# Moving two NF4 steps, four weight splits and two query sums around the first attention steps of a fused cross-attention and feed-forward kernel

## The chip, the cores and the metric

The kernel runs on one core of one Trainium2 chip. The metric is the device time of one launch in microseconds (us). The core has a matrix engine (PE, with its weight loads shown apart as PEld), a vector engine (DVE), a scalar engine (ACT), GpSimd (POOL) and a queue that only issues DMA transfers (SP). Each engine works through its own instructions in the order in which the program emits them, and waits where an operand or a buffer is not ready.

## The reference

Eight sequences of 128 rows and 512 columns pass through one transformer block. Cut to what matters:

```python
# x, ctx: (8, 128, 512); 32 query heads share 8 key/value heads; head size 128
q = rope((layernorm(x) @ Wq).reshape(b, t, 32, 128))
k = rope((ctx @ Wk).reshape(b, t, 8, 128))
v = (ctx @ Wv).reshape(b, t, 8, 128)
logits = 30 * tanh(einsum(q, k) * 0.0884 / 30)     # grouped heads: 4 queries per key head
weights = softmax(where(mask, logits, -1e30))
x = x + (weights @ v).reshape(b, t, 4096) @ Wo
# feed-forward with weights that are quantized and dequantized (NF4, blocks of 64) on the way
dq = lambda w: NF4_CODE[searchsorted(bounds, w / absmax)] * absmax
h = silu(layernorm(x) @ dq(w1).T) * (layernorm(x) @ dq(w2).T)      # 1376 hidden
x = x + h @ dq(w3).T
```

## The kernel before

Every matrix product is made of three matmuls on operands that are split into a rounded part and a remainder (`split`: ACT casts the high part, line 155; DVE or POOL subtracts to get the low part, line 156; `product`, line 172, issues for each pair of operands high x low, high x high, low x high).

The program is one long list written out in the order of Python's loops; no scheduler reorders it. It has four stretches.

- **The head**, the loop over `tiles` with index n from 0 to 35 (line 631): key, value and first query projections, one PE tile each. Beside them run the layer norm of x, its transposes, and from n = 15 on the NF4 stream.
- **The attention steps**, the loop over i from 0 to 63 (line 762). A step i takes one of eight sequences and one of eight key/value heads (`where`). In it are queued on PE, in this order: the query projection of a later step (`q_proj`, bank "q"), the output projection of step i-3 (`project`), the transposes of the attention result of step i-2 (`turn`, tile `pt_a`, bank "q"), the products with the values of step i-1 (`values`, tile `pv`) and the scores of step i (`scores`, tile `pl`). Steps 0 to 2 are special: step 0 has two query projections (tiles 1_0 and 1_1), step 1 has one (1_2) and step 2 has one (1_3); step 3 has none. `project` begins in step 3.
- **The gate and up products** of the feed-forward (line 859) and **the down products** (line 872).

The NF4 work is a generator, `quantize`. One unit of it is one bound: ACT compares (line 196, 128x1024) and DVE accumulates (line 202, or 200 for the first bound of a block). `pump(n)` adds n to a credit and runs the stream until the credit is used, so that the order of the stream never changes, only where in the program its parts stand. On the way the stream issues loads of weights and of scales (`load`, `begin`, line 265 and 275), the reduction of the block maxima (`find`, lines 177 to 179), a normalization on POOL (line 206) and a closing product on DVE (line 280).

The query projection ends in `rope`: two copies on ACT (lines 463 and 464), a product with the cosine on DVE (line 465), a product with the sine on POOL (line 466) and the sum (line 467). For the second set of queries (u = 1: tiles 1_0 to 1_3) the cosine product is written back into the PSUM bank, and the sum runs on DVE and reads that bank; so the bank is free only when the sum is done. There are two banks with the tag "q", used in turn, in program order: 1_0, 1_1, 1_2, 1_3, then `pt_a` of step 2, `pt_a` of step 3, and so on. `pt_a` of step 2 thus takes the bank of tile 1_2, and `pt_a` of step 3 that of tile 1_3.

`q_proj` returns a function that emits the copies and products of `rope`; that one returns the sum as another function. In steps 1 and 2 the copies and products are emitted at the step's start (`later = [f() for f in later[:1]]`), and the sum after `scores`.

The four slices of the output weights of head group 0 (`wo` 0 to 3) are loaded ahead of the loop by `load_o(0, g)` and split when their entry in `due` comes up at the end of a step. The loads of later weights reuse their raw buffers, three with the tag "raw": the load of the first projection weights of the next group (`raw_wq` 1_0, issued in step 0, split at the end of step 2) waits until `wo` 1 is split, the next two for `wo` 2 and 3.

Of the kernel before, what the change touches and what calls it, by code (L numbers as in the profile page):

```python
# [23 lines left out]
G = NH // NKV  # L24
# [38 lines left out]
def block_kernel(ctx: ExitStack, tc: tile.TileContext, x, ctxt, mask, wq, wk, wv, wo, w1, w2, w3, w12t, w3_t,  # L63
                 rope_tab, nf_bias, out):
    nc = tc.nc
    V, S, Q, E = nc.vector, nc.scalar, nc.gpsimd, nc.tensor
# [9 lines left out]
    def bank(tag, name):  # L76
        shape = [P, 1024 if tag == "pv" else 512]
        return ps.tile(shape, F32, tag=tag, name=name, bufs=2 if tag == "q" else 1)[:, :512]
# [75 lines left out]
    def split(hi, lo, src, engine):  # L154
        S.copy(hi, src)  # L155
        engine.tensor_tensor(lo, src, hi, ALU.subtract)  # L156
# [54 lines left out]
    class Down(Unit):  # L211
# [30 lines left out]
        def store(self, h):  # L242
            pool, tag, bufs = (f1, "w3t", 8) if h < 8 else (nf, "nf_t", 2) if h < 10 else (xp, "wide", 2)
            t = w3t[h] = pool.tile([P, 2, KT, P], F32R, tag=tag, name=f"w3t_{h}", bufs=bufs)
            own = t.rearrange("p i k c -> p i (k c)")[:self.p].rearrange("p i (c e) -> p i e c", e=4)
            split(own[:, 0], own[:, 1], self.part(self.w, h).rearrange("p (e c) -> p e c", e=4), Q)
# [158 lines left out]
    def pump(n):  # L405

        credit[0] += n
        while credit[0] > 0:
            credit[0] -= next(stream, n + credit[0])
# [7 lines left out]
    def end_store():  # L417
        if stored:
            stored.pop()()
# [7 lines left out]
    with ExitStack() as c1:  # L427
# [11 lines left out]
        def stage(src, shape, name):  # L439
            if early:  # L440
                raw = early.pop(0)
            else:
                raw = raw_pool[-1].tile([P, 512], F32, tag="raw", name=f"raw_{name}", bufs=3 if len(raw_pool) > 1 else 4)
            if len(shape) == 3:
                raw = raw.rearrange("p (k n) -> p k n", k=shape[1])
            nc.sync.dma_start(raw, src)
            return raw
# [21 lines left out]
        wqt, todo = {}, {}  # L469

        def load_q(kv, g):
            wqt[kv, g], todo["q", kv, g] = columns(wq, kv * G + g, f"wq_{kv}_{g}")

        def q_proj(u, g):
            kv, half = divmod(u, 2)
            if g == 0:
                qr[u] = a1.tile([P, 4, G, T], F32, tag="qr", name=f"qr_{u}", bufs=2)
            pq = bank("q", f"pq_{u}_{g}")
            w, t = wqt[kv, g], xT[half]
            product(pq, [((w[:, 0, k], w[:, 1, k]), (t[:, 0, k], t[:, 1, k])) for k in range(KT)])  # L480
            return lambda: rope(qr[u][:, :, g, :], pq, cosq, sgnq, f"q{u}_{g}", V if u < 2 else None, u == 1)


        with ExitStack() as c3:
# [110 lines left out]
            def advance(n):  # L595

                while True:
                    while loads and (early or len(ready) < 4) and loads[0][0] < n + 7:
                        when, what, i, j = loads.pop(0)
                        ready.append((when, load[what](i, j)))  # L600
                    if not ready or ready[0][0] > n:
                        return
                    ready.pop(0)[1]()
# [27 lines left out]
            for n, (what, i, j) in enumerate(tiles):  # L631
                done = evac() if evac else None
                evac = make[what](i, j)
                if last:
                    last()
                last = done
                advance(n)
                end_store()
                for f in plan[n]:
                    f()  # L640
                if 9 <= n < 19:
                    store()
                if n >= 33:
                    store("wo")
                if n >= 15 and n != 17:
                    pump(1)
            last()
            evac()()
            for f in plan[len(tiles)]:
# [7 lines left out]
        def load_o(kv, g):  # L657
            h = kv * G + g
            raw = stage(wo[h * HD:(h + 1) * HD], [P, D], f"wo_{kv}_{g}")
            t = wot[kv, g] = at.tile([P, 2, D], F32R, tag="wo", name=f"wo_{kv}_{g}", bufs=8)  # L660
            todo["o", kv, g] = lambda: split(t[:, 0], t[:, 1], raw, Q if kv else V)

        def load_kv(kv):
            for half in range(2):
                krt[kv, half] = at.tile([P, 512], F32, tag="kr", name=f"krt_{kv}_{half}", bufs=4)
                nc.sync.dma_start(krt[kv, half], kr_d[kv, half])
            vt[kv] = at.tile([P, B, HD + 1], F32, tag="v", name=f"vt_{kv}")
            nc.sync.dma_start(vt[kv][:, :, :HD], v_d[kv])
            Q.memset(vt[kv][:, :, HD:], 1.0)

        def where(i):
            u, bb = divmod(i, 4)
            return u, u // 2, (u % 2) * 4 + bb, bb

        def scores(i):
            u, kv, b, bb = where(i)
            pl = bank("s", f"pl_{i}")
            E.matmul(pl, krt[kv, u % 2][:, bb * T:(bb + 1) * T], qr[u][:, bb].rearrange("p g t -> p (g t)"),  # L678
                     start=True, stop=True)
            th = at.tile([P, 512], F32, tag="th", name=f"th_{i}", bufs=3)  # L680
            S.activation(th, pl, AF.Tanh, scale=ATTN_MULT / CAP)  # L681
            S.activation(th, th, AF.Exp, scale=CAP)  # L682
            em[i] = th.rearrange("p (g t) -> p g t", g=G)
            Q.tensor_tensor(em[i], em[i], mt.unsqueeze(1).to_broadcast([P, G, T]), ALU.mult)  # L684

        def values(i):
            u, kv, b, bb = where(i)
            ad[i] = at.tile([P, G, HD], F32, tag="ad", name=f"ad_{i}")
            pv = ps.tile([P, G, 256], F32, tag="pv", name=f"pv_{i}", bufs=1)
            for g in range(G):  # L690
                E.matmul(pv[:, g, :HD + 1], em[i][:, g], vt[kv][:, b], start=True, stop=True)  # L691
            rs = tp.tile([P, G], F32, tag="rs", name=f"rs_{i}")
            V.reciprocal(rs.unsqueeze(2), pv[:, :, HD:HD + 1])
            V.tensor_tensor(ad[i], pv[:, :, :HD], rs.unsqueeze(2).to_broadcast([P, G, HD]), ALU.mult)
# [14 lines left out]
        for g in range(G):  # L709
            load_o(0, g)  # L710
# [41 lines left out]
                V.tensor_tensor(hT[half, h // 4][:, h % 4], sg, pu, ALU.mult)  # L752
            return later

        due = {0: [("o", 0, 0), ("o", 0, 1)], 1: [("o", 0, 2), ("o", 0, 3)]}
        xn = {}

        def turned(ks, tags):
            for f in [normal2(k, xn[k], tag) for k, tag in zip(ks, tags)]:
                f()  # L760

        for i in range(N):
            u, kv, b, bb = where(i)
            s8 = i % 8
            if kv + 1 < NKV:
                if s8 == 0:
                    load_kv(kv + 1)
                if s8 < 4:
                    load_q(kv + 1, s8)
                else:  # L770
                    load_o(kv + 1, s8 - 4)
                due.setdefault(i + (2 if i < 4 else 1), []).append(("q" if s8 < 4 else "o", kv + 1, s8 % 4))
            tiles = {0: (0, 1), 1: (2,), 2: (3,), 3: ()}.get(i, (bb,)) if u + 1 < 2 * NKV else ()
            later = [q_proj(u + 1, g) for g in tiles]
            later = [f() for f in later[:1]] + later[1:]
            if i == 0:
                later.pop(0)()
            if i > 3:
                store()
                end_store()  # L780
            pump(1.5 if 2 < i < 58 else 1 if i == 58 else 0)
            if 0 <= i - 3:
                project(i - 3)
            if i in (59, 61):
                ln = LayerNorm((i - 59, i - 58), f"y{i - 59}")
            if 0 <= i - 2:
                turn(i - 2)
            if 59 <= i < 63:
                ln.sums(i - 59)
            if 0 <= i - 1:  # L790
                values(i - 1)
            scores(i)
            if i == 0:
                later = [later[0]()]
            if i == 61:
                xn.update({k: pair.rows(k, "xn") for k in (0, 1)})
            for f in later:
                f()
            pump(1.65 if 2 < i < 58 else 2 if i == 58 else 1 if i < 2 else 0)
            if i == 62:  # L800
                turned((0, 1), "qq")
            if i in (60, 62):
                ln.finish(Q)
                pair = ln
            for k in due.pop(i, ()):
                todo[k]()
            if i >= 61:
                load_w12(i - 61)
# [63 lines left out]
    for b, i in down:  # L872
# [5 lines left out]
        for h in range(4 * i, min(NHT, 4 * i + 4)):  # L878
            m = min(P, H - h * P)
            t, s = w3t[h].rearrange("p i k c -> p i (k c)"), hs[b, i]  # L880
# [7 lines left out]
        elif i == 2:  # L888
            o = f1.tile([P, D], F32, tag="o", name=f"o_{b}", bufs=4)
# [41 lines left out]
```

## Time and profile before

| what | value |
|---|---|
| median of 3 runs | 789.06 us (788.82 to 789.34) |
| the profiled execution | 790.01 us, of which the span from its first to its last instruction is 788.2 us |
| PE busy | 778.0 us, 99% of the span |
| DVE, ACT, POOL busy | 627.9, 586.4 and 466.4 us |
| line 202 (DVE), line 196 (ACT) | 1196 and 1115 ns each on average |
| line 467 on POOL, line 684 on POOL | 1295 and 1310 ns each on average |
| mean granted PE clock | 0.998 |

PE's busy share counts pipelined matmuls whose ends are modelled, so a matmul that stalls in the array looks busy; where a stretch matters, the start times of its instructions say more than the share. Times given as positions are microseconds from the start of the span.

### The profile page before, as it was taken

Reading aid. Unit: us, or ns where it says so; the run is one execution under the profiler, and the core shown is the slowest. Engines: PE = TensorE matmul, PEld = TensorE weight load, DVE = VectorE, ACT = ScalarE, POOL = GpSimd, SP = SyncE. Lnnn points to the kernel's source line nnn. Section 1 sums busy time; section 2 is a strip of 40 time slices with the busy share of each in tenths; the row PEclk is TensorE's granted clock in tenths of the full one; section 3 lists DMA queues with packets and bytes.
Section 4 is the critical chain, followed back from the end, with each engine's and each line's share of the span. In section 5 each row is a group of like instructions: output and inputs, shape, how many; then the busy total and the mean of one; then the engine's idle time right before and its main releaser. Section 6 shows DMA issues by size and latency. Waiting matters only on the chain. (4 is left out here: it accounts for less than half of the span.)

```text
span 788.2 us, 11198 instructions
## 1 busy us (share of the span) xinstructions
PE 778.0 (99%) x3737; PEld 627.3 (80%) x3737; DVE 627.9 (80%) x840; ACT 586.4 (74%) x821; POOL 466.4 (59%) x411
## 2 busy tenths in 40 slices
PE   8999998999999999999999999999999999999998
PEld 6788886778777878778787877888778888888877
DVE  5767777888888887888888878879878688888981
ACT  7358667989796978879797979898732678778840
POOL 3568544688787878777797877878652223232100
PEclk9999999999999999999999999999999999999999
DMA  7966735355437344526337432414133235652011
GB/s 228 300 195 195 214 105 154 108 143 176 89 121 206 135 107 121 174 55 218 103 100 203 131 94 94 125 65 134 43 119 107 57 108 157 186 162 53 5 54 54
DMA packets 73329, 102.44 MB, mean 130 GB/s; under 512 B 7832, under 2 KB 42840, under 8 KB 73272
## 3 DMA queue, kind: packets, MB, share of 16 engines
q1 hardware_dynamic: 70104, 90.19, 38.2%
q0 software_dynamic: 3168, 11.54, 4.7%
q8 instruction: 30, 0.49, 0.3%
q14 instruction: 27, 0.22, 0.1%
HBM read 79.32 MB, written 22.38 MB: 129 GB/s over the span
## 5 line engine op out<-in xcount | busy, mean ns | idle before, releaser
L202 DVE SCALAR_TENSOR_TENSOR nc_w<-nm_w,nc_w 128x1024 f32<-128x1024 bf16 (+1 forms) x238 | 284.6, 1196 | 60.2 <-ACT nm_w L196 49.8
L196 ACT ACTIVATE nm_w<-w_w,bias 128x1024 bf16<-128x1024 f32 (+1 forms) x255 | 276.2, 1115 | 14.9 <-DVE nc_w L202 7.9
L172 PE MATMUL pq<-xT,wq 128*128 128x512 f32 x768 | 209.3, 422 | 0.0
L172 PE MATMUL po<-wo,aT 128*128 128x512 f32 x768 | 190.1, 396 | 0.0
L172 PEld LDWEIGHTS pq<-xT,wq 128*128 128x128 f32 x768 | 143.9, 188 | 55.9 <-issue 24.4
L172 PEld LDWEIGHTS po<-wo,aT 128*128 128x128 f32 x768 | 143.8, 189 | 34.5 <-issue 2.9
L684 POOL TENSOR_TENSOR th<-th,mt 128x512 f32<-128x512 f32 x64 | 83.8, 1310 | 87.9 <-ACT th L682 80.0
L466 POOL TENSOR_TENSOR rs_q<-rs_q,sgnq 128x512 f32<-128x512 f32 x64 | 82.9, 1295 | 14.7 <-ACT rs_q L464 14.7
L681 ACT ACTIVATE th<-pl 128x512 f32<-128x512 f32 x64 | 38.3, 598 | 53.5 <-PE pl L678 51.3
L467 POOL TENSOR_TENSOR qr<-rc_q,rs_q 128x512 f32<-128x512 f32 x56 | 72.5, 1295 | 0.0
L691 PE MATMUL pv<-vt,th 128*128 128x129 f32 x512 | 67.9, 276 | 0.1
L678 PE MATMUL pl<-qr,krt 128*128 128x512 f32 x128 | 66.4, 601 | 0.0
L172 PE MATMUL pg<-xT,w 128*128 128x512 f32 x264 | 63.7, 390 | 0.0
L172 PE MATMUL pu<-xT,w 128*128 128x512 f32 x264 | 63.5, 389 | 0.0
L691 PEld LDWEIGHTS pv<-vt,th 128*128 128x128 f32 x512 | 62.2, 192 | 0.7 <-POOL th L684 0.7
L172 PE MATMUL pd<-w3t,hs 128*128 128x512 f32 (+3 forms) x297 | 60.8, 366 | 0.4 <-POOL w3t L156 0.4
L172 PEld LDWEIGHTS pd<-w3t,hs 128*128 128x128 f32 (+1 forms) x297 | 51.3, 189 | 9.9 <-POOL w3t L156 0.8
L206 POOL TENSOR_TENSOR w_w<-w_w,s_w 128x1024 f32<-128x1024 f32 (+1 forms) x17 | 39.6, 2329 | 33.0 <-DMA s_w<-scale_d 31.6
L172 PEld LDWEIGHTS pu<-xT,w 128*128 128x128 f32 x264 | 49.6, 188 | 10.3
L172 PEld LDWEIGHTS pg<-xT,w 128*128 128x128 f32 x264 | 49.3, 188 | 10.1
L156 POOL TENSOR_TENSOR w3t<-w_w,w3t 128x512 fp32r<-128x512 f32 (+1 forms) x11 | 17.2, 1564 | 65.7 <-ACT w3t L155 65.7
L155 ACT CAST aT<-pt_a 128x512 fp32r<-128x512 f32 x64 | 36.6, 571 | 24.9 <-PE pt_a L162 24.9
(119 smaller groups left out, 1103.7 us busy)
## 6 DMA issues: line engine op xcount, KB each, us to landing
w12t_d<-dqt SPq DMA_DIRECT2D x22, 512.0 KB
w<-w12t_d POOLq DMA_DIRECT2D x22, 512.0 KB, 4.6
s_w<-scale_d SPq DMA_DIRECT2D x40, 256.0 KB
raw_wq<-in_L_xattn_Wq SPq DMA_DIRECT2D x32, 256.0 KB
raw_wo<-in_L_xattn_Wo SPq DMA_DIRECT2D x32, 256.0 KB
s_w<-scale_d SPq DMA_DIRECT2D x86, 64.0 KB
ws<-in_L_ffn_w SPq DMA_DIRECT2D x20, 256.0 KB
w_w<-in_w12t SPq DMA_DIRECT2D x10, 512.0 KB
```

The source lines that it names most:

```text
L155: S.copy(hi, src)
L156: engine.tensor_tensor(lo, src, hi, ALU.subtract)
L172: E.matmul(out, a, b, start=start and i + j == 0, stop=stop and i == n - 1 and j == 2)
L196: S.activation(m, self.w, AF.Relu, bias=bias[:self.p, i:i + 1], scale=BIG if up else -BIG)
L202: V.scalar_tensor_tensor(self.c, m, step, self.c, ALU.min, ALU.subtract if i == POS[0] else ALU.add)
L206: Q.tensor_tensor(self.w, self.w, self.s, ALU.mult)
L466: Q.tensor_tensor(s, s, every(sgn), ALU.mult)
L467: return lambda: (engine or Q).tensor_tensor(dst, c, s, ALU.add)
L678: E.matmul(pl, krt[kv, u % 2][:, bb * T:(bb + 1) * T], qr[u][:, bb].rearrange("p g t -> p (g t)"), start=True, stop=True)
L681: S.activation(th, pl, AF.Tanh, scale=ATTN_MULT / CAP)
L684: Q.tensor_tensor(em[i], em[i], mt.unsqueeze(1).to_broadcast([P, G, T]), ALU.mult)
L691: E.matmul(pv[:, g, :HD + 1], em[i][:, g], vt[kv][:, b], start=True, stop=True)
```

## The change

The diff moves work and removes none. In the head, `pump` runs two units instead of one at n = 24 and n = 28. The one unit at the end of each of steps 0 and 1 goes, so that the stream stands at the same place from step 2 on. The splits of `wo` 0 and 1, at the end of step 0 before, and of `wo` 2 and 3, at the end of step 1 before, now all stand in step 1: 0 and 1 ahead of `scores`, 2 and 3 at its end. The low parts of 2 and 3 are subtracted on POOL instead of DVE. The sums of tiles 1_2 and 1_3 are emitted straight after `values` instead of after `scores`. `scores` itself holds no DVE instruction.

```diff
@@ head, loop over n
                 if n >= 15 and n != 17:
-                    pump(1)
+                    pump(2 if n in (24, 28) else 1)
@@ load_o
-            todo["o", kv, g] = lambda: split(t[:, 0], t[:, 1], raw, Q if kv else V)
+            todo["o", kv, g] = lambda: split(t[:, 0], t[:, 1], raw, Q if kv or g > 1 else V)
@@
-        due = {0: [("o", 0, 0), ("o", 0, 1)], 1: [("o", 0, 2), ("o", 0, 3)]}
+        due = {1: [("o", 0, g) for g in range(G)]}
@@ loop over i
             if 0 <= i - 1:
                 values(i - 1)
+            if i in (1, 2):
+
+                later.pop(0)()
+                if i == 1:
+                    for _ in range(2):
+                        todo[due[1].pop(0)]()
             scores(i)
...
             for f in later:
                 f()
-            pump(1.65 if 2 < i < 58 else 2 if i == 58 else 1 if i < 2 else 0)
+            pump(1.65 if 2 < i < 58 else 2 if i == 58 else 0)
```

## The prediction

> **What bounds the kernel now.** I read the page first, then PE's waits, then a table of stretches, then the timeline of all engines around the one wait that is long. The page says that PE is busy all along, and the waits of PE say where it is not:
>
> ```profile
> PE 778.0 (99%) x3737; PEld 627.3 (80%) x3737; DVE 627.9 (80%) x840; ACT 586.4 (74%) x821; POOL 466.4 (59%) x411
> ```
> ```profile
> PE pt_a L162 <- DVE qr L467: 2.4, 1, 2.4
> PE warm L91 <- POOL ident masks.py:199: 1.4, 1, 1.4
> ```
>
> All other waits of PE sum to about 3 us in pieces of at most 0.5. The time is PE's queue, and only a change in when PE issues can move it. The one long wait is that of the first `pt_a`, for the sum (L467) of query tile 1_2. The table of stretches, cut at 3.41 us, shows what follows it (columns: stretch, length, busy us of PE, PEld, DVE, ACT, POOL, granted clock, DMA share, GB/s):
>
> ```profile
> 123.92:127.33 3.41, 2.99 (x12) 2.13 (x12) 3.41 (x4) 3.34 (x6) 2.21 (x2) 1.00 0.00 0
> 127.33:130.74 3.41, 1.38 (x13) 1.41 (x14) 3.38 (x6) 2.81 (x6) 2.07 (x2) 1.00 0.71 183
> 130.74:134.15 3.41, 3.41 (x8) 1.66 (x7) 3.38 (x7) 1.49 (x3) 0.39 (x2) 0.50 0.66 184
> 134.15:137.57 3.42, 3.42 (x22) 2.98 (x22) 2.54 (x3) 2.92 (x4) 2.36 (x2) 1.00 0.12 25
> ```
>
> PE worked 1.38 of 3.41 us, and in the next 3.41 us the granted clock is 0.50. DVE meanwhile is full. The timeline shows with what:
>
> ```profile
> 121.76 1.27 POOL L466 TENSOR_TENSOR rs_q<-rs_q,sgnq 128x512 f32<-128x512 f32 x1
> ...
> 123.68 1.22 DVE L202 SCALAR_TENSOR_TENSOR nc_w<-nm_w,nc_w 128x1024 f32<-128x1024 bf16 x1
> 123.91 3.00 PE L172 MATMUL pq<-xT,wq 128*128 128x512 f32 x12
> ...
> 124.81 2.39 DVE L156 TENSOR_TENSOR wo<-raw_wo,wo 128x512 fp32r<-128x512 f32 x2
> ...
> 125.12 1.53 POOL L466 TENSOR_TENSOR rs_q<-rs_q,sgnq 128x512 f32<-128x512 f32 x1 [2.08 <-ACT rs_q L464]
> 126.61 1.71 POOL L684 TENSOR_TENSOR th<-th,mt 128x512 f32<-128x512 f32 x1
> 127.12 0.69 DVE L465 TENSOR_TENSOR pq<-pq,cosq 128x512 f32<-128x512 f32 x1
> ...
> 128.53 0.68 DVE L467 TENSOR_TENSOR qr<-pq,rs_q 128x512 f32<-128x512 f32 x1
> ...
> 129.36 0.63 PE L162 MATMUL pt_a<-ident,ad 128*128 128x128 f32 x4 [2.44 <-DVE qr L467]
> ...
> 131.60 4.69 PE L172 MATMUL po<-wo,aT 128*128 128x512 f32 x12
> ```
>
> One NF4 unit and two `wo` splits (123.68 to 127.12) stand on DVE ahead of the rope of tile 1_2.
>
> **Part 1: what is taken out from ahead of the wait.** PE up to tile 1_3 (start 123.91) hangs on the sum of 1_1 at 123.07, itself after POOL's L466 of 121.76; nothing of the change stands before these. Undisturbed, a tile takes 2.85 (109.49 to 112.34), so PE is free for `pt_a` at 126.75. New ACT order: copies of 1_2 when PE has made it, 121.93 to 123.10; two casts of `wo` (0.6 each); tanh and exp of step 1 to 125.53; the other two casts to 126.55; copies of 1_3 126.95 to 128.12. New DVE order: L465 123.68 to 124.38, L693 and L694 to 125.18, the sum of 1_2 once POOL's L466 (123.17 + 1.28 = 124.45) is done: 125.10 to 125.78. The bank is free 0.9 before PE asks. Gain: 129.36 - 126.75 = 2.61. The next late thing could be pv of step 1, on L684: 125.60 + 1.29 = 126.89, wanted at 127.19, so it holds by 0.3.
>
> **Part 2: from this `pt_a` to the next.** Before: 129.36 to 136.13, 6.77. Undisturbed it is 4.52: 1.79 from `pt_a` to the next long group (143.82 to 145.61 in step 4) plus 2.73 of `po` (148.78 to 151.51). The excess of 2.25 is half of 3.41 us at clock 0.50, 1.7, and waiting of `po` for the low part of aT (L156, 132.62 to 133.30). In the new order PE would idle about 1.2 of 3.41 us at most (below); the start of the kernel has a stretch (4.46 to 7.87) with 2.64 busy of 3.41 at clock 1.00. I take it that the clock stays.
>
> [...]
>
> **Part 3: what is late next.** DVE and POOL hinder each other when DVE subtracts two SBUF operands: the two `wo` splits at 124.81 took 2.39 together, 0.69 and then 1.7 beside POOL's L466, and POOL's L684 right behind took 1.71 instead of 1.29. The second split ended 0.55 after L466, and L684 1.13 after the split. So they go one after the other. New order from 125.60: POOL L684 to 126.89; DVE `wo` 0 asked for at 125.70, done 127.44; POOL `wo` 2 done 128.57; DVE `wo` 1 done 129.12; POOL `wo` 3 done 130.25, L466 of 1_3 about 131.6. DVE: L465 of 1_3 129.04 to 129.73, low part of aT 129.65 to 130.33, L693 and L694 to 131.1, the sum of 1_3 131.65 to 132.35. PE: `pt_a` 126.75, pv 127.19, pl 128.08, first `po` 128.8, its third matmul waits for aT to 130.4, ten at 0.228 remain: free at 132.66; the bank of 1_3 is free at 132.5. [...] Both give **132.6 for the second `pt_a`**, an excess of 1.33 instead of 2.25, and a gain of 136.13 - 132.6 = **3.5**. Bounds: with POOL's three pieces at 1.29 and nothing between, 126.89 + 3.87 + 0.85 = 131.6, gain 4.5; with each at 1.71, the sum comes at 132.9 and L684 of step 2, a fourth piece, at 133.7, so that pv starts 0.4 late: gain 2.8. I take 3.5, from the rows of the same pairing.
>
> **Part 4: the moved load.** `raw_wq` 1_0 now waits for `wo` 1 until 129.12 (issued at 127.22 before). The load of this size issued at 136.54 shows in the DMA share of 137 to 139 and not after: 2.5 at most, so it lands by 131.6. ACT's cast then waits 1.2, which holds up behind it two L196, the cast of aT and tanh of step 3; POOL's split of it ends near 134.25. PE's next query tile starts at 134.4, and needs the low part third. Without that margin it would cost what it is late, one to one. Everything from there to the end shifts: ACT waited for PE's scores in 54 of 64 steps (51.3 us together), so it has slack in each, and the tail is `pd` on PE with 0.4 of waiting.
>
> **Part 5: the head.** Two more units at n = 24 and 28: 2 x (L196 1.15 + L202 1.22). They bring forward a reduction (1.21), the POOL normalization (2.40), L280 (1.21) and the DMAs of scales and `ws` on SP. Cover: between 72 and 112 PE waits for nothing; ACT has gaps of 0.6 to 1.7 before most copies, DVE of 0.8 to 1.5; POOL stands idle from 91.1 to 95.8, where the normalization goes; SP from 101.6 to 111.2, where the scales' load of step 0 goes, ahead of no waiting load. A value tile's bank is asked for again 2 tiles later, and the copy of n = 24 ends at 81.2 instead of 80.6, wanted at 85.7. Cost 0; up to 4.7 if nothing of it were covered; a gain is excluded, since PE has no wait there.
>
> **Sum.** The profiled execution has a span of 788.2 and a time of 790.0, 1.8 around it; the median of the runs is 0.95 below. Span 784.7, profile 786.5, median 789.06 - 3.5 = **785.5**. What a measurement here can tell from no change is 0.2%, 1.6 us: 787.5 to 790.6.
>
> **Rivals.**
> 1. *The clock halves all the same*, since the idle of 1.2 (or another cause) suffices. For it: no run here shows the limit between 2.64 and 1.38 us of work per stretch. Against: the clock fell exactly once, behind the one long wait. It gives back 1.7: 787.3. Chance 0.10, half of it counted as no change.
> 2. *Slower: ACT stands in step 2 behind the load of `raw_wq` 1_0.* After landing, the cast, two L196, an L202 and L705 (4.7 together) must be done before PE's second `po` at 137.57; so 3.7 from issue to landing cost nothing, and each us more costs one. [...] For: the load is issued 1.9 later than before, and the page's 512 KB loads on POOL's queue take 4.6. Against: the DMA share above. Chance 0.07.
> 3. *The head's two units are not covered.* One pair exposed (2.4) gives 787.9, both 790.2, no change either way. For: at 115.25 a weight load waits 0.32 for L465, so there the head is tight. Against: there the number of units is the same as before. Chance 0.05.
> 4. *The change does not do what it says*: the wait has another end than L467 and stays: 789. The releaser is named and the bank's order bears it out. Chance 0.01.
>
> **How the numbers follow.** The forecast has 0.77, with a range of its own of 784.5 to 786.3 (gains 4.5 to 2.8). To hold 8 in 10 it must reach rival 1 with some spread: 784.4 to 787.8. Faster: 0.77 + 0.05 = 0.82. No change: 0.05 + 0.05 + 0.01 = 0.11. Slower: 0.07.
>
> **What would show it.** Right: the wait of `pt_a` for L467 of 2.4 is gone, the first `pt_a` starts near 126.8, no stretch at clock 0.50 after the start, the second `pt_a` near 132.6, and `po` before it has a hole of about a microsecond ended by aT's L156 or, at `pt_a`, by L467; the head's PE times up to 118 agree within 0.3. Wrong: a clock of 0.50 near 131 (rival 1), ACT waiting for a DMA at the wq cast beyond 133 (rival 2), PE's first score later than 118.1 (rival 3), or a shift at the second `pt_a` that is not kept at the last `pd`.

## The result, and the profile after

The changed kernel takes 786.20 us in the median (785.79 to 786.97, 6 runs), the kernel before on the same chips 789.27 (788.82 to 789.84, 6 runs): a ratio of 0.9959, with a 95% interval of 0.9949 to 0.9969. That is 3.1 us less, where 3.5 was forecast. The profiled execution took 786.97, its span 785.2 (788.2 before).

PE's waits, the kernel after (what waited, for whom: us in total, times, longest):

```profile
PE warm L91 <- POOL ident masks.py:199: 1.4, 1, 1.4
PE pk L172 <- DVE rc_k L465: 0.9, 2, 0.7
PE po L172 <- DVE aT L156: 0.7, 1, 0.7
```

The wait of `pt_a` for L467 is gone; a wait of `po` for aT's low part has come. The same stretches as before:

```profile
123.92:127.33 3.41, 3.38 (x16) 2.54 (x16) 3.38 (x6) 2.87 (x7) 2.37 (x3) 1.00 0.03 8
127.33:130.74 3.41, 2.70 (x17) 1.76 (x16) 3.38 (x6) 2.93 (x5) 3.41 (x3) 1.00 0.26 61
130.74:134.15 3.41, 3.41 (x21) 2.93 (x22) 2.29 (x3) 2.67 (x5) 3.41 (x3) 1.00 0.51 170
```

No stretch at 0.50. In the first two stretches DVE is as full as before (3.38), and POOL now works without a break from 127.1 to 134. The timeline after, all engines, the rows that answer to those of before:

```profile
122.11 2.69 POOL L466 TENSOR_TENSOR rs_q<-rs_q,sgnq 128x512 f32<-128x512 f32 x2
...
125.43 0.68 DVE L467 TENSOR_TENSOR qr<-pq,rs_q 128x512 f32<-128x512 f32 x1
...
126.03 3.33 DVE L156 TENSOR_TENSOR wo<-raw_wo,wo 128x512 fp32r<-128x512 f32 x2
...
127.10 0.60 PE L162 MATMUL pt_a<-ident,ad 128*128 128x128 f32 x4
127.10 3.41 POOL L156 TENSOR_TENSOR wo<-raw_wo,wo 128x512 fp32r<-128x512 f32 x2
...
129.89 0.68 DVE L156 TENSOR_TENSOR aT<-pt_a,aT 128x512 fp32r<-128x512 f32 x1
...
130.62 2.58 PE L172 MATMUL po<-wo,aT 128*128 128x512 f32 x10 [0.71 <-DVE aT L156]
...
133.03 0.60 PE L162 MATMUL pt_a<-ident,ad 128*128 128x128 f32 x4
```

The sum ends at 126.11, a microsecond before PE asks for the bank. What is late next is aT's low part, behind two DVE splits that take 3.33 together.

Positions in a span move by some tenths from run to run: the first scores (`pl`) start between 117.7 and 118.6 in the twelve profiles here, and the difference is there from the first `pt_x` on, which stands 53.3 to 53.4 ahead of them in all. So the experiments are compared by one distance, from the start of the first scores to the start of the second `pt_a`: 136.13 - 118.12 = 18.0 before, 133.03 - 118.45 = 14.6 after. From the second `pt_a` to the end of the span, all twelve profiles lie between 652.1 and 652.3: whatever happens in steps 0 to 3 is kept to the end in full, and nothing is given back.

### The profile page after: what moved, and what is told of

Same layout as the page of the kernel before. It is cut to its first block, busy times and chain, and to the rows that moved or that the text cites. A ratio compares the mean times of both kernels' runs of the same rounds, so it can differ in the third digit from the quotient of the medians.

```text
span 785.2 us, 11201 instructions
## 1 busy us (share of the span) xinstructions
PE 777.0 (99%) x3737; PEld 627.3 (80%) x3737; DVE 628.3 (80%) x838; ACT 586.3 (75%) x821; POOL 469.1 (60%) x413
## 5 line engine op out<-in xcount | busy, mean ns | idle before, releaser
L202 DVE SCALAR_TENSOR_TENSOR nc_w<-nm_w,nc_w 128x1024 f32<-128x1024 bf16 (+1 forms) x238 | 284.6, 1196 | 57.0 <-ACT nm_w L196 46.1
L196 ACT ACTIVATE nm_w<-w_w,bias 128x1024 bf16<-128x1024 f32 (+1 forms) x255 | 276.0, 1115 | 15.9 <-DVE nc_w L202 7.9
L684 POOL TENSOR_TENSOR th<-th,mt 128x512 f32<-128x512 f32 x64 | 83.5, 1305 | 87.2 <-ACT th L682 78.7
L466 POOL TENSOR_TENSOR rs_q<-rs_q,sgnq 128x512 f32<-128x512 f32 x64 | 82.5, 1289 | 15.0 <-ACT rs_q L464 14.8
L467 POOL TENSOR_TENSOR qr<-rc_q,rs_q 128x512 f32<-128x512 f32 x56 | 72.5, 1294 | 0.0
```

What stands on the lines that cost most here:

```text
L196: S.activation(m, self.w, AF.Relu, bias=bias[:self.p, i:i + 1], scale=BIG if up else -BIG)
L202: V.scalar_tensor_tensor(self.c, m, step, self.c, ALU.min, ALU.subtract if i == POS[0] else ALU.add)
L466: Q.tensor_tensor(s, s, every(sgn), ALU.mult)
L467: return lambda: (engine or Q).tensor_tensor(dst, c, s, ALU.add)
```

## The experiments

The theory: PE waits in steps 1 to 3 for a chain of DVE and POOL instructions, and each piece ahead of the sum of 1_2 and of aT's low part is paid for. Rivals: the moved NF4 units alone do it; the half clock is a cost of its own, or has a cause of its own.

| kernel | distance | PE waits by its list: for the first `pt_a`, for aT in `po` | ratio to before, 95% interval |
|---|---|---|---|
| before | 18.0 | 2.4, none listed (half clock) | 1 |
| changed | 14.6 | none, 0.7 | 0.9959 (0.9949 to 0.9969) |
| nf4_only | 15.9 | 1.3, 0.5 | 0.9976 (0.9966 to 0.9985) |
| splits_only | 16.6 | none, 0.5 (high part) and 1.3 | 0.9992 (0.9983 to 1.0001) |
| sum_behind_splits | 15.1 | 1.3, none | 0.9966 (0.9954 to 0.9978) |
| filled_wait | 17.6 | 0.2, 1.1 | 0.9999 (0.9990 to 1.0007) |
| wo_all_dve | 15.8 | none, 1.9 | 0.9983 (0.9974 to 0.9992) |
| no_pool_splits | 13.8 | none, none | 0.9951 (0.9937 to 0.9964) |
| one_ahead | 13.8 | none, none | 0.9952 (0.9939 to 0.9964) |
| interleaved | 13.6 | none, none | 0.9948 (0.9936 to 0.9960) |

**nf4_only**, the NF4 units alone:

```diff
-                    pump(1)
+                    pump(2 if n in (24, 28) else 1)
...
-            pump(1.65 if 2 < i < 58 else 2 if i == 58 else 1 if i < 2 else 0)
+            pump(1.65 if 2 < i < 58 else 2 if i == 58 else 0)
```

> Only the two NF4 units move into the head; splits and sums stand as in the kernel before. Worked from rows: without the two L202 the sum of 1_2 ends near 127.1, so the first pt_a waits 0.5 instead of 2.6, the low part of aT is no longer behind splits that alternate with POOL, and the second pt_a comes near 132.0 (136.13 before, 133.03 in the changed kernel, of which 0.35 was already there at the head's end). Theory 1 (the whole change is needed because each DVE piece ahead of the sum counts): clock at 1.0, time 785 to 786.5, some of the gain missing. Rival (the NF4 units alone make the gain, and the move of the splits to step 1 and to POOL costs): 785.2, that is 0.6 to 1.0 below the changed kernel's 786.2, with the wait for aT of 1.1 shrunk below 0.7.

Measured: 787.73, distance 15.9, and not the 13.9 that a second `pt_a` at 132.0 meant (132.0 - 118.12). Neither side of the expectation held in its numbers. The timeline of DVE and POOL in this kernel shows why:

```profile
123.28 2.38 DVE L156 TENSOR_TENSOR wo<-raw_wo,wo 128x512 fp32r<-128x512 f32 x2
123.67 1.45 POOL L466 TENSOR_TENSOR rs_q<-rs_q,sgnq 128x512 f32<-128x512 f32 x1 [1.03 <-ACT rs_q L464]
...
127.00 0.68 DVE L467 TENSOR_TENSOR qr<-pq,rs_q 128x512 f32<-128x512 f32 x1
127.60 2.36 DVE L156 TENSOR_TENSOR wo<-raw_wo,wo 128x512 fp32r<-128x512 f32 x2
127.80 1.61 POOL L466 TENSOR_TENSOR rs_q<-rs_q,sgnq 128x512 f32<-128x512 f32 x1 [0.98 <-ACT rs_q L464]
```

I had counted 0.7 for each split; but in both pairs the second one meets POOL's L466 and takes 1.8. The two units give 2.1 of the change's 3.4, and the splits must give the rest.

**splits_only**, the splits and the sums alone; the edit is the change without the two `pump` lines.

> Only the splits and the sums move; the two NF4 units stay in steps 0 and 1. Worked from rows: the sum of 1_2 ends near 127.0 since two splits left its front and one L202 stays, first pt_a 0.4 late; the second L202 then stands ahead of aT's low part, third po matmul near 131.4, second pt_a near 133.7 or 2.4 earlier than before: 786.9, clock at 1.0. Rival (splits and sums give nothing by themselves): 789.3.

Measured: 788.61, distance 16.6 (133.7 - 118.12 = 15.6 expected). The first `pt_a` waits for nothing, but L202 of step 1 stands after two splits that take 3.09 and ahead of aT, and `po` waits 1.3 for it:

```profile
126.64 3.09 DVE L156 TENSOR_TENSOR wo<-raw_wo,wo 128x512 fp32r<-128x512 f32 x2
...
129.66 1.22 DVE L202 SCALAR_TENSOR_TENSOR nc_w<-nm_w,nc_w 128x1024 f32<-128x1024 bf16 x1
...
131.39 0.67 DVE L156 TENSOR_TENSOR aT<-pt_a,aT 128x512 fp32r<-128x512 f32 x1
```

The distance falls by 1.4; in the times the interval just includes no change. One reason may be the clock: eight of the eleven executions, the profiled one among them, have a mean granted clock of 1.000 and take 788.49 on average, 1.2 below the kernel before (789.66); the other three have 0.997 or 0.998 and take 789.99. 2.1 and 1.4 add up to 3.5: the two parts work on the same chain and do not replace each other.

**sum_behind_splits**, the changed kernel with one line moved:

```diff
             if i in (1, 2):
-                later.pop(0)()
                 if i == 1:
                     for _ in range(2):
                         todo[due[1].pop(0)]()
+                later.pop(0)()
```

> The changed kernel with the sum of 1_2 emitted behind the two wo splits of step 1 instead of ahead of them. If the order on DVE is what frees the bank: the second split must wait for POOL's L684, the sum ends near 128.6, the first pt_a is 1.6 to 1.9 late, but the aT wait behind it shrinks; second pt_a near 133.2 to 133.5 if the clock stays (786.5) and about 1.7 later if a wait of this length already halves it (788.0). Rival (the place of the sum is without effect, the moved NF4 units are all): 786.2 and no wait at the first pt_a.

Measured: 786.89, distance 15.1, 1.3 of waiting for the first `pt_a`, none for aT, and the clock at 1.00. Close to what was expected without the clock, with a shorter wait (1.3, not 1.6 to 1.9). The place of the sum is worth 0.5 of distance, no more, because the wait moves from one place to the other: the same two splits are paid ahead of the sum or ahead of aT. (The profile puts this wait down to ACT's L464, which ended 0.02 after DVE's L467 in this kernel; two releasers that close can't be told apart by the view, and it is the same in nf4_only. In the changed kernel `pt_a` starts at 127.10 and this L464 only at 127.89, so it is not L464 that `pt_a` needs.)

**filled_wait**, the kernel before with work for PE in the wait:

```diff
+            if i == 2:
+                idle = bank("wo", "idle")
+                for k in range(10):
+                    E.matmul(idle, xT[1][:, 0, k % 4, :P], xT[1][:, 0, k % 4], start=True, stop=True)
             if 0 <= i - 2:
                 turn(i - 2)
```

> The kernel before with ten matmuls of 128x512 on xT queued on PE ahead of the first pt_a, into the idle bank of po; their result is never read. They fill 2.3 us of the 2.6 us wait and shorten nothing. If the idle of PE made the clock fall: no stretch at 0.50 near 131, second pt_a near 134.4 instead of 136.1, time 787.6, 1.7 below the kernel before. [...]

Measured: 789.54, the same as before (0.9990 to 1.0007), distance 17.6. The stretches after the fill and PE's timeline:

```profile
126.88:130.29 3.41, 3.22 (x20) 2.55 (x19) 3.38 (x7) 2.94 (x6) 2.11 (x2) 1.00 0.57 164
130.29:133.70 3.41, 2.28 (x11) 1.32 (x10) 3.38 (x6) 2.21 (x5) 1.24 (x2) 1.00 0.71 171
```
```profile
126.63 2.43 PE L789 MATMUL idle<-xT 128*128 128x512 f32 x10
129.25 0.63 PE L162 MATMUL pt_a<-ident,ad 128*128 128x128 f32 x4 [0.19 <-DVE qr L467]
...
131.06 1.03 PE L172 MATMUL po<-wo,aT 128*128 128x512 f32 x2
133.23 2.57 PE L172 MATMUL po<-wo,aT 128*128 128x512 f32 x10 [1.14 <-DVE aT L156]
```

The expectation was half right. The clock did stay at 1.00, in all eleven executions (in 12 of 50 of the kernel before), so PE's idle time was what made it fall in that kernel. But the fall was nearly free: `po` still waits for aT until 133.23, because aT depends on DVE and not on PE's clock. In the kernel before, the half clock (130.74 to 134.15) lay over that wait, as aT's low part ended only at 133.30:

```profile
132.62 0.68 DVE L156 TENSOR_TENSOR aT<-pt_a,aT 128x512 fp32r<-128x512 f32 x1
```

Only the 0.85 us of half clock behind it can count, and half of that is about the 0.4 by which the distance fell.

**wo_all_dve**, the changed kernel without the move to POOL:

```diff
-            todo["o", kv, g] = lambda: split(t[:, 0], t[:, 1], raw, Q if kv or g > 1 else V)
+            todo["o", kv, g] = lambda: split(t[:, 0], t[:, 1], raw, Q if kv else V)
```

> The changed kernel with wo 2 and 3 subtracted on DVE like 0 and 1. From the first score to the second pt_a it was 14.6 us in the changed kernel, 18.0 before. If DVE subtractions of SBUF operands must wait for a POOL instruction that runs, and stand ahead of aT's low part: all four splits end near 130.5, aT near 131.8, distance 15.7, time 1.1 above the changed kernel (787.3 on its runs). Rival (POOL's splits are what holds DVE up, so DVE alone is quicker): distance 14 or less, 785.6.

Measured: 787.8, distance 15.8, `po` 1.9 late. As expected to 0.1 in the distance: POOL's part of the change is worth 1.2 there, though it costs DVE something, which the next kernel measures.

**no_pool_splits**, the changed kernel without POOL's two subtractions:

```diff
+            if kv == 0 and g > 1:
+                Q.memset(t[:, 1].bitcast(F32), 0.0)
+                todo["o", kv, g] = lambda: S.copy(t[:, 0], raw)
```

> The changed kernel without the two subtractions of wo 2 and 3 (their low parts are zeroed on POOL long before, so these parts are left out of the result). If the second DVE split took 1.75 us because POOL's split ran: it takes 0.7, aT's low part comes 0.7 earlier, distance from first score to second pt_a 13.9 instead of 14.6, and 785.5. Rival (a DVE split beside other engines is simply that slow): 1.7 again and distance 14.5.

Measured: 785.66, distance 13.8. The instructions on tile `wo` (duration in ns, least, median and most), first in the changed kernel, then in this one:

```profile
L156 DVE TENSOR_TENSOR wo<-raw_wo,wo x2: 1655/1704/1754, 126.0 to 127.6; 128x512 fp32r<-128x512 f32 x2
L156 POOL TENSOR_TENSOR wo<-raw_wo,wo x2: 1711/1720/1730, 127.1 to 128.8; 128x512 fp32r<-128x512 f32 x2
```
```profile
L156 DVE TENSOR_TENSOR wo<-raw_wo,wo x2: 680/1176/1671, 125.6 to 127.2; 128x512 fp32r<-128x512 f32 x2
```

The first DVE split still meets L684 (line 688 in this kernel) and takes 1671; the second finds POOL idle and takes 680. The wait for POOL is inside the instruction's duration and in no list of waits.

**one_ahead**, a different order of the two DVE splits:

```diff
             if i in (1, 2):
+                if i == 1:
+                    todo[due[1].pop(0)]()
                 later.pop(0)()
                 if i == 1:
-                    for _ in range(2):
-                        todo[due[1].pop(0)]()
+                    todo[due[1].pop(0)]()
```

> The changed kernel with only one of the two DVE splits ahead of the sum of 1_2 and the other behind it. The first split falls into POOL's idle time before L684 of step 1 (about 1 us), so it costs 0.7 and not 1.65; the sum still frees the bank before PE asks; all behind it is 0.5 earlier, POOL's chain with it. Distance 13.9 to 14.1, time 785.5 to 785.7 on the changed kernel's runs. Rival (POOL's chain of two splits, L466 and L684 is the bound whatever DVE does): distance 14.5, no change.

Measured: 785.79, distance 13.8. The first split now takes 0.68 (125.17, POOL idle), the second 1.20.

**interleaved**: as one_ahead, and in step 2 `turn` stands ahead of the rope of 1_3, with the DVE subtraction of `wo` 3 straight behind it.

> As one_ahead, and in step 2 the transposes of pt_a stand ahead of the rope of 1_3, with the low part of wo 3 on DVE right behind aT's. Takes aT out from behind L465 and one split out of POOL's chain. If both chains were the last waits: distance 13.5, 785.1, close to the 13.2 that PE alone needs. Rival (the split of wo 3 collides with POOL again, or the query sum comes late): distance 14 to 14.5, no better than one_ahead.

Measured: 785.36, distance 13.6, PE waiting nowhere in steps 0 to 3:

```profile
126.44 0.60 PE L162 MATMUL pt_a<-ident,ad 128*128 128x128 f32 x4
...
128.23 3.32 PE L172 MATMUL po<-wo,aT 128*128 128x512 f32 x12
131.38 0.60 PE L162 MATMUL pt_a<-ident,ad 128*128 128x128 f32 x4
```

From `pt_a` to `po` it is 1.79 here and 2.03 in one_ahead and no_pool_splits, where the weight loads of `po` (PEld, a list of its own) still wait for aT. The last two runs put interleaved beside the changed kernel on one chip:

> The changed kernel itself, on one chip with the next run. 3.0 to 3.5 below the kernel before; distance from the first score to the second pt_a 14.5 to 14.6.

> The kernel interleaved, on one chip with the changed kernel. If its distance of 13.6 against 14.6 is kept to the end: 0.9 to 1.0 below the changed kernel, 4.0 to 4.5 below the kernel before. Rival (the gain is given back behind step 3): no difference from the changed kernel.

Measured: 786.23 for the changed kernel (785.94 to 786.70; ratio 0.9959, 0.9947 to 0.9972) and 784.89 for interleaved (784.75 to 786.12; 0.9944, 0.9930 to 0.9957), with distances of 14.6 and 13.6. The 1.0 of distance shows in the medians, 1.3, though the two intervals overlap. Against the kernel before the gain is clear; against the changed kernel it rests on the distance, which came out the same in two profiles of each.

## Why the prediction was right, and where it was not

Positions in this section are taken back by 0.33, the later start of the first scores in the profile after.

- **Part 1, the wait of the first `pt_a`.** Right. The sum ends at 125.78 (125.78 forecast) and `pt_a` starts at 126.77 (126.75).
- **Part 2, "the excess of 2.25 is half of 3.41 us at clock 0.50, 1.7, and waiting of `po`".** Both the excess and its split were wrong. The undisturbed 4.52 took `po` from a step in which it stands behind another long group (2.73); behind the scores, as here, its 12 matmuls take 3.15 in interleaved, and the way from `pt_a` to `pt_a` is 4.94 with no wait of PE in it. So the excess before was 1.8. With the clock held up (filled_wait) the distance falls by 0.4, not by 1.7; the rest was the wait for aT, behind the second L202 and the splits of `wo` 2 and 3. The forecast did not suffer, because its 132.6 was walked from row to row, and neither 4.52 nor 1.7 is a term of it.
- **The clock.** A wait of 2.44 stood ahead of the 3.41 us at 0.50, and filling it kept the clock at 1.00. Rival 1 did not happen: all eleven executions of the changed kernel have a mean granted clock of 1.000. What it would have cost there was not measured. In the kernel before the clock took 0.4 and not 1.7; the last section has two kernels in which it seems to have taken more.
- **Part 3, DVE and POOL in turns.** Right: the two DVE splits end at 129.03 (129.12 forecast), POOL's two at 130.18 (130.25), the third `po` matmul starts at 130.29 (130.4), the second `pt_a` at 132.70 (132.6). It was aT that decided and not the bank, as in the forecast (PE free at 132.66, the bank at 132.5): the sum of 1_3 ended at 132.48 in the profile, 0.55 ahead of the second `pt_a`. The row that the forecast went by, a split that ends 0.55 after POOL's instruction, holds throughout: in all 19 places of the twelve profiles where a DVE split of `wo` started with 0.6 us or more of a POOL instruction left, it ended 0.55 after that instruction, whether it took 1.20 or 1.79. In no_pool_splits one such split took 680 ns with POOL idle, the other 1671 ns behind POOL's L684 (line 688 there).
- **Part 4, the moved load.** Right. ACT waits 0.73 for it (1.2 forecast), PE not at all.
- **Part 5, the head.** Right, the cost is nothing: from the first `pt_x` to the first scores it is 118.12 - 64.72 = 53.4 before and 118.45 - 65.13 = 53.3 after. Rival 3 is out, and so are rivals 2 (by Part 4) and 4 (the wait for L467 is gone).
- **The size.** The distance fell by 3.4, where 3.5 was worked out; the medians by 3.1. The difference is within the interval (2.4 to 4.0). The two profiled executions differ by 3.0, since the first scores start 0.33 later in the profile after; by the spread of these starts (117.7 to 118.6) that can't be put down to the change.

My expectations for nf4_only and splits_only were 2.0 and 1.0 too short in distance. That for nf4_only failed where Part 3 had held: I priced splits at 0.7 in an order in which they meet POOL. In splits_only both splits ahead of L202 meet POOL too (1.42 and 1.75); the expectation does not say what I had put for them.

## What to carry to other kernels

When one engine is the bound and waits once, cost the whole chain behind that wait by walking each engine's queue in program order, since removing the wait only uncovers the next one: PE alone needs 13.6 here (8.65 to the first `pt_a` and 4.94 from there, as in interleaved, and not the 13.2 of my expectation), so 4.4 of lateness became 1.0. A subtraction of two SBUF operands on DVE was cheap here (0.7) in POOL's idle time and dear (1.2 to 1.8) beside POOL's work, so a better place in the order can be worth as much as taking POOL's work away (one_ahead and no_pool_splits both reach 13.8). And a half clock that lay over another wait cost little here (0.4, not 1.7): test it by filling the idle time before counting it as a gain.

## What the runs showed of the hardware

Leaving out the first and the last microseconds of the span, two of the twelve profiles have a half clock. It lasts 3.41 us in both, and the 3.41 us ahead of it hold little work of PE: 1.38 us in the kernel before, 1.43 us in one_ahead, where PE waits 2.0 for ACT's cast in the head:

```profile
4.21:7.63 3.42, 1.43 (x7) 0.76 (x7) 1.34 (x3) 1.50 (x3) 0.00 (x0) 1.00 0.93 306
7.63:11.04 3.41, 3.41 (x9) 2.63 (x9) 1.77 (x3) 2.79 (x5) 1.60 (x2) 0.50 1.05 396
```

In one_ahead too it cost nothing that can be seen: the first scores start at 118.20, inside the spread of the others.

So little work did not always bring it on: in wo_all_dve, where PE waits 1.94 for aT, a stretch of 3.41 us holds 1.47 us of work, and the mean granted clock of that execution is 1.000:

```profile
127.94:131.35 3.41, 1.47 (x7) 0.53 (x5) 3.41 (x5) 2.65 (x6) 2.55 (x2) 1.00 0.54 165
```

What sets this stretch apart from the other two, no run shows. One kernel can have both: of 50 executions of the kernel before 28 have a mean granted clock of 0.998 and 12 one of 1.000, while all eleven of filled_wait have 1.000.

What the half clock costs differed between kernels. In the kernel before, the executions at 0.998 take 0.1 less, 0.2 more and 1.1 more than those at 1.000 in its three sets of runs (the last, three against three). In splits_only the three at 0.997 or 0.998 take 1.5 more than the eight at 1.000, and in wo_all_dve the five at 0.997 or 0.998 take 1.2 more than the five at 1.000. In the profiles of these two kernels, both at 1.000, PE's list has waits for aT alone in steps 1 to 3, so a half clock behind them might have no further wait to lie over. That was not shown: no trace of the executions at 0.997 or 0.998 is kept.
